# Three float32r passes for a float32 product in the first phase of a two-layer attention kernel

The kernel runs on one core of one Trainium2 chip. The metric is the device time of one execution in microseconds (us); medians are over several executions, and a span is the time between the first and the last instruction of the one execution that was profiled.

## The reference

Two attention layers over an image batch, 8 images of 512 channels and 1024 positions, all float32. The change touches only the q, k, v product of layer 0.

```python
# layer 0
h = group_norm(x)                                    # 32 groups
qkv = einsum('oc,bct->bot', qkv_w, h) + qkv_b        # 1536 x 512 weights
q, k, v = split(qkv.reshape(b * 8, -1, T), 3)        # 8 heads of 64
q, k, v = fake_quant(q), fake_quant(k), fake_quant(v) # 8 bits; the scale comes from
                                                      # min and max of the WHOLE tensor
w = softmax(q^T k / sqrt(64)); a = v w^T
x = x + proj_w a + proj_b
# layer 1: group norm, q/k/v, one head of 512, projection, residual (cut)
```

The quantisation needs the minimum and maximum over the whole batch before any value can be rounded. So the kernel has two phases: phase 1 computes q, k and v of all images, stores them in DRAM and keeps their extremes; phase 2 reads them back, quantises, and does the attention of layer 0 and all of layer 1, image by image. Between them stands a chain: reduce the extremes, compute the scales, load and quantise the first head, find its row maxima (from score matmuls called `sm`), and only then the first score matmul whose result is used (`st`). I call the stretch from the end of the last v matmul to the first `st` the boundary.

## The kernel before

Phase 1 takes one image at a time: statistics and normalisation (`group_norm`, with two tiny averaging matmuls), 64 products of q and k, 32 of v. Weights of layer 1 are merged (`wq` with `wk`, `wv` with `wp`, matmuls `mg`, and small ones for the biases, `mgb`) on TensorE right after phase 1.

```python
for b in range(B):
    if b + 1 < B:
        load_x(b + 1)
    ...                                              # cut: loads of layer 1 weights
    group_norm(xs.pop(b), hn, V_GN0W, V_GN0B, f"a{b}")
    for h in range(HEADS):
        ps = big_ps(f"qkps_{b}_{h}")                 # PSUM, 1024 columns
        for hf in range(NH):
            for cc in range(CC):                     # 4 blocks of 128 channels
                nc.tensor.matmul(ps[:, bass.ts(hf, 512)],
                    lhsT=wqkv[:, cc, h*3*CH : h*3*CH + 2*CH],
                    rhs=hn[:, cc, bass.ts(hf, 512)], start=(cc == 0), stop=(cc == CC - 1))
        nc.vector.tensor_scalar(qk, ps, vec[...], None, ALU.add, ALU.max, accum_out=qkmax[...])
        nc.vector.tensor_reduce(qkmin[...], qk, AX.X, ALU.min)
        nc.sync.dma_start(qk_d[b][h], qk)
    for t in range(NT):
        ...                                          # cut: v, the same with operands swapped
        nc.vector.tensor_add(vt, ps, vb)
        ...                                          # cut: max, min, store
merge_weights()
```

## Time and profile before

4405.49 us in the median of three runs (4390.6 to 4419.51). The stages, from the table of stages that the prediction shows:

| stage | us | length | what sets its end |
|---|---|---|---|
| start, to the first q/k product | 0 to 31.4 | 31 | loads, statistics of image 0 |
| phase 1 | 31.4 to 761.1 | 730 | TensorE, 94% busy |
| boundary | 761.1 to 810.0 | 49 | the merge to 797, beside which the chain of scales is done by 781; then the first maxima |
| phase 2 | 810.0 to 4403.8 | 3594 | TensorE, 92% busy |

One thing about the reading of TensorE rows: records overlap with their neighbours (616 ns in the mean where they start every 429), so a stream is timed from start to start.

### The profile page before, as it was taken

How to read it: one execution, taken by the hardware profiler on the slowest of the kernel's cores; microseconds unless marked ns; L12 is line 12 of the kernel's file. 1: busy time of each engine (PE TensorE's matmuls, PEld its weight loads, DVE VectorE, ACT ScalarE, POOL GpSimd, SP SyncE). 2: the span in 40 equal slices, each digit the busy share in tenths (PEclk: the TensorE clock that was granted, in tenths of full speed). 3: DMA queues.
4: the chain of work that ended last, by engine and by line, in shares of the span. 5: the costliest groups of instructions: out<-in, count | busy, mean ns of one | idle time of the engine just before them, and what ended most of it. 6: DMA issues, size and time to landing. Idle time of an engine off the chain costs nothing.

```text
span 4403.8 us, 26651 instructions
## 1 busy us (share of the span) xinstructions
PE 4049.7 (92%) x10432; PEld 1529.5 (35%) x10432; DVE 1782.4 (40%) x2621; ACT 1051.7 (24%) x1129; POOL 109.0 (2%) x102
## 2 busy tenths in 40 slices
PE   7899999889998899989988998999989989998999
PEld 3344444323432343234322432243224422442244
DVE  4544444554234523452355224522452244324422
ACT  0000000342133312431243123312331243113411
POOL 0000000000000000000000000000000000000000
PEclk9999999899998999899989998999889988999899
DMA  4222212100010101010101010101010100000000
GB/s 186 93 95 91 86 73 85 53 20 29 0 48 15 34 0 48 15 34 0 43 20 34 0 43 20 34 0 43 15 35 4 38 20 15 24 28 26 1 0 19
DMA packets 69678, 161.92 MB, mean 37 GB/s; under 512 B 23216, under 2 KB 23216, under 8 KB 68912
## 3 DMA queue, kind: packets, MB, share of 16 engines
q1 hardware_dynamic: 64032, 135.05, 8.5%
q10 hardware_dynamic: 5520, 25.17, 1.5%
q8 instruction: 82, 1.34, 0.1%
q14 instruction: 44, 0.36, 0.0%
HBM read 92.56 MB, written 67.11 MB: 36 GB/s over the span
## 4 chain that ended last, share of the span: by engine, by line
PE 83%; DVE 7%; ACT 4%; issue 3%; DMA 2%; POOL 0%; SPq 0%; POOLq 0%; ACTq 0%; DVEq 0%
PE av L384 20%; PE o L511 10%; PE s L477 10%; PE qkps L208 9%; PE sm L323 7%; PE qk L452 5%; PE st L395 5%; PE v2ps L464 5%; PE pj L432 4%; PE vps L226 4%; DVE negm L330 3%; PE tp L503 1%; DMA sums<-un 1%; ACT pt L403 1%; DVE q_aug L350 1%
## 5 line engine op out<-in xcount | busy, mean ns | idle before, releaser
L384 PE MATMUL av<-pt,vq 128*65 128x512 f32 x2048 | 1102.9, 666 | 70.6 <-ACT pt L403 70.6
L330 DVE TENSOR_REDUCE negm<-sm 128x1 f32<-128x1024 f32 x512 | 626.3, 1224 | 892.4 <-PE sm L323 891.6
L403 ACT ACTIVATE pt<-st,esc 128x1024 f32<-128x1024 f32 x512 | 569.6, 1114 | 931.7 <-PE st L395 930.4
L384 PEld LDWEIGHTS av<-pt,vq 128*65 128x65 f32 x2048 | 294.5, 151 | 602.1 <-issue 425.5
L208 PE MATMUL qkps<-h,wqkv 128*128 128x512 f32 x1024 | 462.9, 616 | 30.4 <-ACT h L158 30.3
L477 PE MATMUL s<-h,q 128*128 128x512 f32 x1024 | 443.4, 592 | 0.0
L511 PE MATMUL o<-pT,v 128*128 128x512 f32 x1024 | 442.9, 593 | 0.3 <-DVE pT L505 0.3
L323 PE MATMUL sm<-k_aug,q_aug 64*128 64x512 bf16 x1024 | 341.3, 417 | 69.3 <-DVE negm L330 36.7
L395 PE MATMUL st<-q_aug,k_aug 67*128 67x512 bf16 x1024 | 347.7, 415 | 54.0 <-DVE q_aug L350 44.0
L208 PEld LDWEIGHTS qkps<-h,wqkv 128*128 128x128 f32 x1024 | 201.9, 198 | 285.4 <-issue 253.0
L511 PEld LDWEIGHTS o<-pT,v 128*128 128x128 f32 x1024 | 193.9, 190 | 244.5 <-issue 241.1
L477 PEld LDWEIGHTS s<-h,q 128*128 128x128 f32 x1024 | 193.3, 190 | 237.2 <-issue 237.2
L452 PE MATMUL qk<-h,wqk 128*128 128x512 f32 x512 | 240.7, 634 | 29.6 <-ACT h L158 29.6
L158 ACT ACTIVATE h<-h,vec 128x1024 f32<-128x1024 f32 x64 | 68.3, 1137 | 748.4 <-DVE h L154 748.4
L323 PEld LDWEIGHTS <-q_aug 64*128 64x128 bf16 x1024 | 65.1, 96 | 502.4 <-issue 427.4
L432 PE MATMUL pj<-ao,wp 128*128 128x512 f32 x512 | 221.8, 593 | 0.0
L464 PE MATMUL v2ps<-wvp,h 128*128 128x512 f32 x512 | 221.0, 592 | 0.0
L226 PE MATMUL vps<-wqkv,h 128*128 128x512 f32 x512 | 221.0, 592 | 0.0
L471 DVE COPY v<-v2ps 128x512 f32<-128x512 f32 x64 | 44.3, 692 | 415.0 <-PE v2ps L464 415.0
L489 ACT ACTIVATE p<-s,nm 128x1024 f32<-128x1024 f32 x64 | 71.4, 1115 | 546.2 <-DVE nm L486 546.2
L519 DVE SCALAR_TENSOR_TENSOR x<-o,ub,x 128x512 f32<-128x512 f32 x64 | 48.1, 751 | 376.7 <-PE o L511 376.7
L216 DVE TENSOR_SCALAR_CACHE_REDUCE qk<-qkps,vec 128x1024 f32<-128x1024 f32 x64 | 82.1, 1283 | 252.3 <-PE qkps L208 252.3
(113 smaller groups left out, 2207.3 us busy)
## 6 DMA issues: line engine op xcount, KB each, us to landing
qk_d<-qk SPq DMA_DIRECT2D x64, 512.0 KB, 2.6
rqk<-qk_d SPq DMA_DIRECT2D x64, 512.0 KB, 3.5
x<-in_x_dram SPq DMA_DIRECT2D x32, 512.0 KB, 6.1
v_d<-v SPq DMA_DIRECT2D x64, 256.0 KB, 2.0
x<-in_x_dram ACTq DMA_DIRECT2D x8, 2048.0 KB, 7.8
rv<-v_d SPq DMA_DIRECT2D x32, 512.0 KB, 4.2
out_dram<-x SPq DMA_DIRECT2D x16, 1024.0 KB, 4.2
wraw<-in_w_res_dram ACTq DMA_DIRECT2D x4, 1024.0 KB, 8.9
```

The source lines that it names most:

```text
L208: nc.tensor.matmul(ps[:, bass.ts(hf, 512)], lhsT=wqkv[:, cc, h * 3 * CH : h * 3 * CH + 2 * CH], rhs=hn[:, cc, bass.ts(hf, 512)], start=(cc ...
L226: nc.tensor.matmul(ps, lhsT=hn[:, cc, bass.ts(t, P)], rhs=wv_cols[:, cc, :, 2, :], start=(cc == 0), stop=(cc == CC - 1),)
L323: nc.tensor.matmul(ps[:, bass.ts(hf, 512)], lhsT=q_aug[a][0:CH, bass.ts(t, P)], rhs=k_aug[a][0:CH, bass.ts(hf, 512)], start=True, stop=True,)
L330: nc.vector.tensor_reduce(negm[g][:, t : t + 1], ps, AX.X, ALU.max, negate=True)
L384: nc.tensor.matmul(av[hf][0 : CH + 1, :], lhsT=vq[b][:, s, h, :], rhs=pt[:, bass.ts(hf, 512)], start=(s == 0), stop=(s == NT - 1),)
L395: nc.tensor.matmul(ps[:, bass.ts(hf, 512)], lhsT=k_aug[a][:, bass.ts(s, P)], rhs=q_aug[a][:, bass.ts(hf, 512)], start=True, stop=True,)
L403: nc.scalar.activation(pts[s], ps, AF.Exp, scale=esc)
L432: nc.tensor.matmul(ps, lhsT=wp0[:, cc, bass.ts(oc, P)], rhs=src[:, cc, :], start=(cc == 0), stop=(cc == CC - 1),)
L452: nc.tensor.matmul(ps[:, bass.ts(hf, 512)], lhsT=wqk[:, cc, bass.ts(oc, P)], rhs=hn[:, cc, bass.ts(hf, 512)], start=(cc == 0), stop=(cc == ...
L464: nc.tensor.matmul(ps, lhsT=hn[:, cc, bass.ts(t, P)], rhs=wvp[:, cc, :], start=(cc == 0), stop=(cc == CC - 1),)
L477: nc.tensor.matmul(ps[:, bass.ts(hf, 512)], lhsT=qt[:, cc, bass.ts(n, P)], rhs=hn[:, cc, bass.ts(hf, 512)], start=(cc == 0), stop=(cc == C ...
L511: nc.tensor.matmul(ps, lhsT=vt[:, m, bass.ts(dc, P)], rhs=pT[:, m, :], start=(m == 0), stop=(m == NT - 1),)
```

## The change

Intent: a float32 matmul makes four passes through the array (the prediction says from where; in the trace it is two records). Split each operand into a high part that float32r is meant to take exactly, and a rest; three such passes, added up suitably, are meant to give a product of the same accuracy. With x = hi + lo, w = wh + wl and E12 = 2^-12, the sum is (1 + E12) (hi wh + lo wl/E12) + (hi - lo/E12) (wl - E12 wh), which multiplies out to x w; the code calls the last two factors `su` and `ws`, and wl/E12 `wd`. Three passes in place of four is 25% off. To hide the splitting and the group norm behind matmuls, phase 1 now goes by halves of an image, with the next half split and the next image normalised while the present one is multiplied. PSUM, where matmuls leave their results, is given to it in another way (3 x 2 banks), and so is SBUF, the memory for operands; the loads and the merge of the layer 1 weights stand in the program after the first row maxima of phase 2.

```diff
+        def split(i, cc):                      # one half image, one channel block
+            nc.scalar.activation(hi, h, AF.Copy, scale=SHRINK)
+            nc.vector.tensor_sub(lo, h, hi.bitcast(F32))
+            nc.vector.scalar_tensor_tensor(
+                su, lo.bitcast(F32), -1.0 / E12, hi.bitcast(F32), ALU.mult, ALU.add)
+        def product(nm, w, x, swap=False):
+            for part in (0, 1, 2):             # hi*wh, lo*wd -> p1_;  su*ws -> p2_
+                for cc in range(CC):
+                    nc.tensor.matmul(p2_ if part == 2 else p1_, lhsT=a_, rhs=b_, ...)
 # q and k: bias on ScalarE out of PSUM, then one fused add and max
+            nc.scalar.activation(t_, p1_, AF.Identity, bias=..., scale=1.0 + E12)
+            nc.vector.tensor_tensor_reduce(out=qk, in0=t_, in1=p2_, op0=ALU.add,
+                                           op1=ALU.max, accum_out=qkmax[...])
 # v: the bias is a row, added on GpSimd
+            nc.scalar.activation(t_, p1_, AF.Copy, scale=1.0 + E12)
+            nc.gpsimd.tensor_tensor(t_, t_, vb, ALU.add)
+            nc.vector.tensor_tensor_reduce(out=vt, in0=t_, in1=p2_, ...)
 # start: the weights are split too, four quarters of 1536 columns
+            nc.scalar.activation(wh[:, cc, :], raw, AF.Copy, scale=SHRINK)
+            nc.vector.tensor_sub(lo, raw, ...); tensor_scalar(wd, ...); scalar_tensor_tensor(ws, ...)
 # loop
-        for b in range(B):  group_norm(...); 8 heads; 8 tiles of v
+        for i in range(B * NH):                # halves
+            for h in range(HEADS):
+                qk_of(i, h)
+                if nxt and h % 2 == 1:
+                    split(i + 1, h // 2)
+                if hf == 0 and h == 1 and b + 1 < B:
+                    norm(b + 1)
+            for j in range(NT // NH):
+                v_of(i, j)
-    merge_weights()
 ...                                            # cut: phase 2 up to its first row maxima
     put_max(0)
+    merge_weights()                            # with its loads, 5 MB
```

## The prediction

> **What bounds the kernel now.** I read the page first, then the same trace cut into stages, then the timeline at the places where two stages meet. The page gives the frame:
>
> ```profile
> span 4403.8 us, 26651 instructions
> PE 4049.7 (92%) x10432; PEld 1529.5 (35%) x10432; DVE 1782.4 (40%) x2621; ACT 1051.7 (24%) x1129; POOL 109.0 (2%) x102
> L208 PE MATMUL qkps<-h,wqkv 128*128 128x512 f32 x1024 | 462.9, 616 | 30.4 <-ACT h L158 30.3
> L226 PE MATMUL vps<-wqkv,h 128*128 128x512 f32 x512 | 221.0, 592 | 0.0
> ```
>
> TensorE is busy for 92% of the span. The change touches only the two matmul lines of phase 1 (L208 for q and k, L226 for v), 462.9 + 221.0 = 683.9 us, so what it can win is a part of that. The program holds 768 such products and the profile counts 1536: one float32 matmul is two records. The table of stages (columns: window, its length, busy time of PE, PEld, DVE, ACT, POOL, granted clock, DMA share, GB/s) says what limits phase 1, and what is beyond it:
>
> ```profile
> 31.40:761.10 729.70, 686.68 (x1565) 304.82 (x1566) 346.82 (x535) 32.96 (x31) 7.06 (x7) 0.96 0.23 89
> 761.10:797.10 36.00, 36.00 (x129) 20.69 (x127) 13.43 (x34) 13.64 (x20) 0.62 (x2) 0.96 0.58 198
> 797.10:810.00 12.90, 8.99 (x26) 2.74 (x26) 11.28 (x17) 0.00 (x0) 0.00 (x0) 0.50 0.00 0
> 810.00:4403.00 3593.00, 3316.87 (x8712) 1200.22 (x8711) 1398.36 (x2006) 1002.64 (x1076) 96.80 (x79) 0.93 0.07 22
> ```
>
> Phase 1 is the first row: TensorE 94% busy, VectorE under half, DMA under a quarter. It is bound by TensorE. The second row is the weight merge, the third the first row maxima, and the fourth (3593 us) is the attention of both layers. The timeline of the last two images shows the seams:
>
> ```profile
> 675.83 57.88 PE L208 MATMUL qkps<-h,wqkv 128*128 128x512 f32 x128 [3.70 <-ACT h L158]
> ...
> 733.54 27.63 PE L226 MATMUL vps<-wqkv,h 128*128 128x512 f32 x64
> ...
> 761.01 27.63 PE L108 MATMUL mg<-wraw 128*128 128x512 f32 x64
> ...
> 788.48 8.71 PE L120 MATMUL mgb<-vec,wraw 128*128 128x1 f32 x64
> ...
> 797.13 1.89 PE L323 MATMUL sm<-k_aug,q_aug 64*128 64x512 bf16 x4
> ```
>
> The v records start at 733.54 and the merge at 761.01, so 64 records take 27.47 us, 429.2 ns from start to start. (The means of 592 and 616 ns overlap, because matmuls are pipelined; the spacing is what counts.) One image is 192 x 0.4292 = 82.4 us, plus 2.8 us because the first records after the pause run at half clock, plus a pause of some 6.9 us for the group norm: 8 x 85.2 + 7 x 6.9 = 730 us, the row above. The merge (36 us) covers the wait for the quantisation scales: TensorE never stops between 733 and 797.
>
> **What the Trainium skill says.** "FP8 and Floating Point Precision", section TensorE Precision Notes: float32 goes through the array in four passes (high and low parts), and one pass works at about 22 bits. "TensorE: Matmul & The Clock Gate", section Back-to-back issue gap: a warm matmul of N columns takes N/2.4 + 2.5 ns. The trace agrees: two passes of 512 in one record are 1024/2.4 + 2.5 = 429.2 ns, exactly what was measured; so one pass should be 512/2.4 + 2.5 = 215.8 ns. The trace supports single passes at that rate, though only for bfloat16: two st matmuls, each with its own weight load, take 0.44 us (855.28 - 854.84). The same page, section LDWEIGHTS, has about P/1.2 ns for P columns, 107 ns for 128. The float32 transposes agree: 24 of them, each with its own 128-column load, start between 1161.08 and 1163.72, every 110 ns. A load for every pass thus fits behind 215.8 ns. "GPSIMD Engine Reference", section 3.1, puts a two-input tensor_tensor at about 2.6 cycles per element, so 512 x 2.6 / 1.2 = 1.1 us for the new bias add; no trace here shows one of that size.
>
> **The change part by part.** *Matmuls.* Each of the 768 products becomes three single passes, 3 x 215.8 = 647 ns instead of 858 ns. An image has 96 products: 62.2 us instead of 82.4 us; eight images 497 us instead of 659 us, a gain of 162 us. This rests on a float32r pass running at one column per cycle, which no record of this trace shows; that is my choice.
>
> *The group-norm pause.* The order of instructions of the changed program puts the statistics of image b+1 into image b's stream, and its two small averaging matmuls a product apart. The seven pauses of 6.9 us and the half-clock starts (2.8 us each) go: 7 x 9.7 = 68 us. In their place VectorE is fuller. Per image, by durations of the present rows: 24 results with a reduction, some 0.76 us each (the 1024-wide L216 takes 1.33 us to the next operation, less 512 elements at 0.96 GHz, 0.53), and 24 minima of 0.60, together 33; 8 splits of two operations (0.61 and 0.69), 10; the norm, 9 to 10. Sum 52 to 56 us against 62.2 of TensorE: 85 to 90%. In the first half of an image, where the norm falls, it is 31 against 31, and three PSUM buffers bridge two products. I charge 1.5 us a time, 12 us in all, for the lag. ScalarE has 24 x 0.59 + 8 x 0.71 + 4 x 1.14 = 24 us per image, GpSimd 8 x 1.1 = 9: neither binds.
>
> *The start.* The weights are split before the first product: per quarter ScalarE 1.5 us, VectorE two 1536-wide operations of (1536 + 151)/0.96 = 1.76 us and one of about 0.95, so 4 x 4.5 = 18 us on VectorE, in line with 11 us of statistics for two images, 3 of normalisation and the first splits; the averaging matmuls of image 1 also precede the first product. VectorE gets its first data at 11 us and is then nearly full for 35 to 40 us: the stream starts at about 50 us instead of 31.4. Cost 19 us.
>
> *The end of phase 1.* From the end of the last v matmul (761.1) to the first st (810.0) it was 49 us, with the merge hidden in the scale chain (761 to 781) and then TensorE still merging until 797. Now the merge stands after the first maxima on TensorE's queue, and the st matmuls stand after the merge. So: scale chain about 23 us (before 20; the last v now passes through GpSimd and a longer VectorE tail), maxima and their transposes 12, merge 36, of which its first 5 us at half clock add 2.5: 73 us. The five 1 MB weight loads are issued as phase 1 ends; at the 198 to 276 GB/s that the trace reaches they take 20 to 27 us, done before the merge wants them at about 35. Cost 73 - 49 = 24 us. After the first st the order on TensorE is the same in both programs, so 3593 us stay.
>
> *Sum.* 50 + 2.7 (cold start) + 497 + 12 = 562 us to the end of phase 1, + 73 = 635 at the first st, + 3594 = 4229 us of span, + 1.7 us by which the median time exceeds the span = 4231. I add 7 us for what a new stage usually leaves unfilled: **4238 us**, 3.8% less.
>
> **The rivals.** (1) *VectorE becomes the bound of phase 1.* For it: 85 to 90% load in an in-order queue; the fused add-and-max may be slower than I took it (if 0.4 us more each, 62 to 66 us per image, or more); GpSimd shares SBUF access with it. Against it: three PSUM buffers and its 48% now. At 68 us per image phase 1 ends near 600: 4275 us. (2) *Weight loads set the pace.* Each pass brings its own load, and the records show 190 ns for a float32 load of 128 columns, near the 216 of a pass. Against it: these 190 ns lie under other matmuls, and the transposes turn one round in 110 ns. At 260 ns a pass an image is 75 us: about 4335 us, within 2%. (3) *A float32r matmul needs two passes.* Then it is 3 x 429 ns a product, 8 x 124 us, and the kernel is slower: about 4720 us. Against it: then there would be nothing to split for. (4) *The gain is as large as it can be:* a start at 46 us, no lag, a boundary of 65 us: 4208 us.
>
> **Range and chances.** Between (4) and a VectorE bound of moderate size the range is 4205 to 4290 us. The 2% mark is 0.98 x 4405.5 = 4317. Rival 1 does not reach it; rival 2 and a combination of a late start with a bad boundary do. Faster by over 2%: 0.86; within 2%: 0.10; slower: 0.04, almost all of it rival 3.
>
> **What would show it.** In the changed profile: one record per product and pass, 2304 in all, at a spacing of 216 ns in the middle of an image (260 or more: rival 2; 429: rival 3); the busy time of phase 1's matmuls about 500 us; no pause above 2 us between images; VectorE at 85 to 90% in phase 1, with no matmul waiting long for its results (at 97% and over, with long waits for it: rival 1); the first product stream at about 50 us, the end of v near 562, the merge after the first sm, the first st near 635, and then 3593 us. A wait of the merge for its weights, or of the first sm for a slow load of q and k behind them, would make the boundary longer than the 73 us and the prediction too low.

## The result, and the profile after

The changed kernel takes 4245.28 us in the median of four runs (4236.1 to 4256.63), the kernel before 4411.98 on the same chip (four runs, 4390.6 to 4419.51). The ratio is 0.9631, 95% interval 0.9587 to 0.9675: faster by 3.7%. Ratios here are the mean time of one kernel's fast runs over that of the other's of the same rounds, so not quite the ratio of the medians quoted. The result passed as correct; how accurate it is was not measured, and the check is not sharp enough to tell (it also passed a kernel with one of the three passes left out, below). The page of the changed kernel:

```profile
span 4239.2 us, 29270 instructions
PE 3875.0 (91%) x11200; PEld 1660.8 (39%) x11200; DVE 1852.0 (44%) x2953; ACT 1216.4 (29%) x1389; POOL 196.5 (5%) x166
```

768 more records on TensorE, yet 175 us less busy time. The table of stages, cut at the first product, the end of v, the start of the merge and the first `st` (columns as in the prediction: window, length, busy time of PE, PEld, DVE, ACT, POOL, granted clock, DMA share, GB/s):

```profile
43.80:580.60 536.80, 529.54 (x2329) 436.38 (x2329) 397.99 (x845) 186.88 (x282) 93.58 (x71) 1.00 0.31 117
580.60:620.00 39.40, 8.99 (x25) 2.70 (x24) 23.07 (x47) 4.58 (x4) 3.44 (x4) 0.55 0.81 319
620.00:658.30 38.30, 38.30 (x130) 22.32 (x130) 1.15 (x3) 4.69 (x8) 0.00 (x0) 0.90 0.00 0
658.30:4239.20 3580.90, 3296.03 (x8713) 1197.50 (x8713) 1398.11 (x2007) 1007.41 (x1084) 96.85 (x80) 0.94 0.07 22
```

Phase 1 fell from 730 to 537 us and is still TensorE's: 99% busy. The boundary grew from 49 to 78 us: 39 us in which TensorE has nearly nothing to do, then 38 us of merge that nothing hides. Phase 2 has the same instructions; its 13 us less are looked at below. In the middle of an image, four passes of one operand a line, the timeline shows:

```profile
149.02 1.07 PE L184 MATMUL qk<-h,wh 128*128 128x512 f32 x4
149.93 1.07 PE L184 MATMUL qk<-h,wd 128*128 128x512 f32 x4
```

From start to start 0.91 us for four passes; from this row to the one at 183.47 us there are 38 such steps, 34.45/38 = 0.9066 us each: 226.6 ns a pass. And the boundary, lines of TensorE, GpSimd and VectorE (the brackets tell the idle time before and who ended it):

```profile
579.68 1.07 PE L184 MATMUL v<-ws,h 128*128 128x512 f32 x4
...
592.91 0.40 POOL L294 PARTITION_ALL_REDUCE exa<-ext  x1 [9.20 <-issue]
...
600.50 1.86 PE L406 MATMUL sm<-k_aug,q_aug 64*128 64x512 bf16 x4 [19.75 <-ACT k_aug L399]
...
607.13 0.75 DVE L386 TENSOR_SCALAR qi<-rqk,qk_rcp 128x1024 f32<-128x1024 f32 x1 [1.19 <-DMA rqk<-qk_d]
609.92 2.14 PE L406 MATMUL sm<-k_aug,q_aug 64*128 64x512 bf16 x4 [7.56 <-DVE negm L413]
...
620.01 28.90 PE L353 MATMUL mg<-wraw 128*128 128x512 f32 x64
648.75 9.66 PE L365 MATMUL mgb<-vec,wraw 128*128 128x1 f32 x64
658.28 1.01 PE L478 MATMUL st<-q_aug,k_aug 67*128 67x512 bf16 x2
```

So: 19.9 us from the last v to the first `sm`, 19.5 us for the first maxima, 38.3 us of merge. In the scale chain, GpSimd's reduction over partitions starts 9.2 us after VectorE has made its input (583.7); no run asks why. In the maxima VectorE's queue has quantising of v and of the next q and k ahead of the maxima, and the second `sm` group waits 7.56 us for it. VectorE stands idle in this for 1.97, 0.70 and 1.19 us, 3.9 in all, until loads of v, q and k have landed, which run beside the weight loads (DMA share 0.81 over the 39 us); the rest is the quantising itself.

Three questions were left for experiments: why a pass takes 226.6 ns where bfloat16 takes 215.8; what each part of the change is worth; and what still stands in phase 1's way. In the table, the times of each trace that are used below (us; "v end" is the end of the last v record, the last two columns are TensorE's busy time in phase 2 and the median time, or the only one of a single run):

| kernel | first product | v end | first st | phase 2 | PE busy in it | median |
|---|---|---|---|---|---|---|
| before | 31.4 | 761.1 | 810.0 | 3593.8 | 3316.9 | 4411.98 |
| after | 43.8 | 580.7 | 658.3 | 3580.9 | 3296.0 | 4245.28 |
| four passes by halves | 26.6 | 693.7 | 762.5 | 3618.3 | 3341.1 | 4387.14 |
| early merge | 45.7 | 587.8 | 631.2 | 3567.7 | 3287.5 | 4240.24 |
| two passes (not exact) | 43.6 | 450.5 | 532.5 | 3611.2 | 3334.5 | 4145.87 |
| after, again | 43.8 | 579.6 | 658.0 | 3600.3 | 3321.7 | 4260.33 |
| both ends | 36.6 | 581.1 | 624.5 | 3591.6 | 3314.7 | 4216.13 |
| no bias add (wrong) | 43.7 | 571.3 | 649.4 | 3626.2 | 3350.8 | 4277.32 |
| add on VectorE | 43.8 | 571.9 | 650.2 | 3633.5 | 3360.3 | 4279.28 |
| add aside (wrong) | 43.8 | 573.6 | 651.1 | 3601.2 | 3321.5 | 4253.89 |
| both ends, add on VectorE | 36.4 | 564.4 | 614.4 | 3592.2 | 3312.8 | 4211.79 |

### The profile page after: what moved, and what is told of

Read it like the earlier page. It is cut to its first block, busy times and chain, and to the rows that moved or that the text cites. A ratio compares the mean times of both kernels' runs of the same rounds, so it can differ in the third digit from the quotient of the medians.

```text
span 4239.2 us, 29270 instructions
## 1 busy us (share of the span) xinstructions
PE 3875.0 (91%) x11200; PEld 1660.8 (39%) x11200; DVE 1852.0 (44%) x2953; ACT 1216.4 (29%) x1389; POOL 196.5 (5%) x166
## 4 chain that ended last, share of the span: by engine, by line
PE 83%; DVE 8%; ACT 4%; DMA 2%; issue 2%; POOL 1%; POOLq 0%; SPq 0%; ACTq 0%; DVEq 0%
PE av L467 21%; PE o L594 10%; PE s L560 10%; PE qk L184 7%; PE sm L406 7%; PE qk L535 6%; PE st L478 5%; PE v2ps L547 5%; PE pj L515 5%; PE v L184 3%; DVE negm L413 3%; DMA sums<-un 1%; PE tp L586 1%; ACT pt L486 1%; ACT vq L447 1%
## 5 line engine op out<-in xcount | busy, mean ns | idle before, releaser
L467 PE MATMUL av<-pt,vq 128*65 128x512 f32 x2048 | 1089.5, 659 | 70.9 <-ACT pt L486 70.9
L478 PE MATMUL st<-q_aug,k_aug 67*128 67x512 bf16 x1024 | 344.0, 411 | 54.2 <-DVE q_aug L433 43.7
L568 DVE TENSOR_REDUCE nm<-s 128x1 f32<-128x1024 f32 x64 | 78.4, 1224 | 233.1 <-PE s L560 233.1
L478 PEld LDWEIGHTS <-k_aug 67*128 67x128 bf16 x1024 | 69.7, 99 | 276.7 <-issue 270.0
L506 POOL PARTITION_BROADCAST bc<-bc x64 | 86.7, 1354 | 1856.5 <-DMA bc<-rs 1082.2
L535 PEld LDWEIGHTS qk<-h,wqk 128*128 128x128 f32 x512 | 103.8, 205 | 160.3 <-issue 130.0
L203 ACT ACTIVATE t<-qk,vec 128x512 f32<-128x512 f32 x128 | 87.4, 688 | 224.6 <-PE qk L184 196.6
```

Source lines behind the costliest of these rows:

```text
L203: nc.scalar.activation(t_, p1_, AF.Identity, bias=vec[:, V_QKB + h : V_QKB + h + 1], scale=1.0 + E12)
L467: nc.tensor.matmul(av[hf][0 : CH + 1, :], lhsT=vq[b][:, s, h, :], rhs=pt[:, bass.ts(hf, 512)], start=(s == 0), stop=(s == NT - 1),)
L478: nc.tensor.matmul(ps[:, bass.ts(hf, 512)], lhsT=k_aug[a][:, bass.ts(s, P)], rhs=q_aug[a][:, bass.ts(hf, 512)], start=True, stop=True,)
L535: nc.tensor.matmul(ps[:, bass.ts(hf, 512)], lhsT=wqk[:, cc, bass.ts(oc, P)], rhs=hn[:, cc, bass.ts(hf, 512)], start=(cc == 0), stop=(cc == ...
```

## The experiments

### e1_probe: streams of matmuls alone

The kernel does nothing but streams of 96 matmul records, each with its own weight load, and copies x to the output.

```diff
+    probe("ra", wr, mr, 96)              # float32r, 512 columns
+    probe("bf", wb, mb, 96)              # bfloat16
+    probe("fp", w, m, 48)                # float32, two records each
+    probe("rhalf", wr, mr, 96, N=256)
+    probe("bhalf", wb, mb, 96, N=256)
+    probe("rnarrow", wr, mr, 96, M=64)   # 64 weight columns
+    probe("rsame", ...); probe("ralone", ...); probe("rb", wr, mr, 96)
```

> The cost of one float32r pass by itself (the kernel computes nothing useful, its output is a copy of x, wrong on purpose). Streams of 96 matmuls back to back, nothing else on the chip: float32r 128x128 by 512 (ra, rb), the same in bfloat16 (bf), float32 (fp, 48), float32r and bfloat16 with 256 columns (rhalf, bhalf), float32r with a 64-column weight (rnarrow), with the same weight every time (rsame), without accumulation (ralone). The changed kernel showed 226.6 ns from start to start where the prediction had 215.8. Theory 1, the weight load of four-byte data sets the pace: rhalf stays above 190 ns, rnarrow falls to 216, bf is 216 to 220. Theory 2, a fixed extra of some 11 ns in each float32r record: rhalf about 120, rnarrow and rsame 226. Theory 3, the stream of four-byte columns is 5% slower: rhalf about 113, fp above 429. Theory 4, the neighbours in the real kernel slow it: ra is 216.

The timeline, one line a stream; a spacing is the difference of two starts over 96:

```profile
24.58 22.12 PE L83 MATMUL ra<-mr,wr 128*128 128x512 f32 x96
46.54 20.89 PE L83 MATMUL bf<-mb,wb 128*128 128x512 bf16 x96
67.27 41.36 PE L83 MATMUL fp<-m,w 128*128 128x512 f32 x96
108.07 12.06 PE L83 MATMUL rhalf<-mr,wr 128*128 128x256 f32 x96
119.98 10.65 PE L83 MATMUL bhalf<-mb,wb 128*128 128x256 bf16 x96
130.39 22.32 PE L83 MATMUL rnarrow<-mr,wr 128*64 128x512 f32 x96
```

bfloat16 takes 215.9 ns and float32r 228.7 in the first stream, 226.9, 226.7 with the same weights every time and with no accumulation. With 256 columns it is 108.4 and 124.1 ns; 64 weight columns take 230.8. So the extra of some 11 to 16 ns does not scale with the columns, and comes neither from the neighbours in phase 1 nor from the accumulation. The kernel's 226.6 ns is what a float32r stream takes by itself.

### e2_four_pass: the structure by halves without float32r

The changed kernel with plain float32 products, no splits, results taken as before (and a third buffer for x).

```diff
-        wh = p1w.tile([P, CC, 3 * C], F32R, name="wh")           # and wd, ws
+        wh = p1w.tile([P, CC, 3 * C], F32, name="wh")
-            for part in (0, 1, 2):
-                for cc in range(CC):
+            for cc in range(CC):
+                nc.tensor.matmul(p1_, lhsT=a_, rhs=b_, ...)       # a_, b_: wh and x
-                    split(i + 1, h // 2)                          # and the weights' split
-            nc.gpsimd.tensor_tensor(t_, t_, vb, ALU.add)
+            nc.vector.tensor_add(vt, p1_, vb)
```

> The new structure of phase 1 (halves of an image, norm of the next image inside the stream, merge in phase 2) with the old float32 matmuls of four passes; no split. If hiding the norm is worth what I predicted (seven pauses of 6.9 us and the half-clock starts of 2.8 us go, 68 us, less about 9 us of waits for the averaging matmuls), phase 1 ends at 33 + 659 + 9 = about 702 us (before: 761), the boundary still costs 77 us, and the time is about 4368 us, 1% under before. Rival: the norm still stops TensorE as long as before because the averaging matmuls stand in its in-order queue; then the time is before plus the 28 us of the longer boundary, about 4440 us.

4387.14 us, ratio 0.9929 (0.9914 to 0.9944), right result.

```profile
26.55 8.97 PE L163 MATMUL qk<-x,wh 128*128 128x512 f32 x16 [4.15 <-ACT x L118]
...
689.66 4.03 PE L163 MATMUL v<-wh,x 128*128 128x512 f32 x9
```

The last v ends at 693.7 where before it was 761.1, 67 us sooner: 63 of them from a shorter stream (729.7 to 667.1 from first product to end of v), which is what hiding the norm is worth, and 5 from an earlier first product. The boundary is 68.8 us, 20 more than before with the merge behind the maxima, and 9 less than in the changed kernel, where I had expected 77. The 9 us lie in one place: GpSimd's reduction over partitions starts 0.1 us after its input here, and 6.3 us after it in the kernel before, 9.2 in the changed one. In those two a memset stands right before it in GpSimd's queue, after the end of v; here GpSimd had been idle for 157 us. Whether that is the reason is not tested. The rest of the distance to the changed kernel, 693.7 - 580.7 = 113 us, is the three passes with all that they need: the stream from first product to v end is 130 us shorter (667.1 to 536.8) and starts 17 us later. The total came out above the 4368 us that I had expected, though v ended sooner than its 702, because phase 2 took 3618 us in this profile.

### e3_early_merge: the merge back into the scale chain

The layer 1 weights are loaded in the last two images into the tiles of x that come free, and merged inside phase 1's block, behind the last v.

```diff
+            if hf == 0 and b + 2 >= B:
+                load_raws(b + 2 - B, p1)
+        merge_weights(ps_p, ps_g)        # after the last v, PSUM of phase 1
 ...
     put_max(0)
-    merge_weights()
```

> The changed kernel with the merge put back to the end of phase 1: the four weights are loaded during the last image into the x buffers that are free by then, and the merge runs while the scales are worked out. If the boundary is long because the merge stands after the maxima, the first st comes 49 to 52 us after the last v matmul instead of 77.7 us, and the time falls by 26 to 28 us to about 4217 us. Also the wait of the first maxima for the v loads (7 us) should go, as no weight load is beside them. Rival: the scale chain and the loads set the boundary, and only those 7 us go: about 4238 us.

```profile
587.68 27.63 PE L156 MATMUL mg<-wraw 128*128 128x512 f32 x64
...
618.70 1.03 PE L411 MATMUL sm<-k_aug,q_aug 64*128 64x512 bf16 x4
...
631.20 0.58 PE L483 MATMUL st<-q_aug,k_aug 67*128 67x512 bf16 x1 [0.35 <-DVE q_aug L438]
```

The boundary is 43.5 us in place of 77.7: the merge covers the scale chain again, and the maxima take 12 us. Their loads now have the DMA to themselves, and also the time of the merge to land; the run does not tell the two apart. Phase 1 ends 7 us later: its first product comes 1.9 us later, and half of the small `mgb` matmuls slipped into it (3.6 us). The first `st` comes at 631.2, 27 us sooner. The time is 4240.24 us, ratio 0.9618 (0.9601 to 0.9636), which does not stand out from the changed kernel's 0.9631 (0.9587 to 0.9675): I had expected 26 to 28 us less, but 27 us are 0.6%, and phase 2 differs by as much from execution to execution (the five times go from 4200.77 to 4255.94, and the profile is of the fastest).

### e4_two_pass: is VectorE near?

The second of the three passes is dropped (not an exact product).

```diff
-            for part in (0, 1, 2):
+            for part in (0, 2):
```

> The changed kernel without the second of the three passes (wrong result on purpose). Where is VectorE's own limit? If TensorE still bounds phase 1: 768 passes of 226.6 ns less, 174 us, phase 1 ends near 407 us and the time is about 4071 us. If VectorE takes over, as its 398 us of busy time from 44 us on say: phase 1 ends at 445 to 465 us, long waits of matmuls for VectorE's results appear, time about 4120 us.

256 x 3 records of 226.6 ns are 174 us of TensorE; the last v came 130 us sooner. Then TensorE waits, as the view of waits shows (waited for: us in total, times, longest):

```profile
PE v L184 <- DVE qkmax L207: 20.3, 6, 3.4
```

VectorE is 94% busy from 43.6 to 450.5 us (382.9 of 406.9), as the second branch of the expectation had it. So VectorE could carry phase 1 in 407 us, 130 us below the 537 of the changed kernel. VectorE as the bound was not near.

### e5_after_again: the changed kernel unedited, on the chip of the runs below

```diff
 (no edit)
```

> The changed kernel once more, unedited, so that it and the kernel with both ends mended share a chip, and to see whether the length of phase 2 belongs to the kernel or to the execution. By the traces so far phase 1 and the boundary repeat to a microsecond while phase 2, with the same instructions, took from 3568 to 3618 us, and its TensorE busy time from 3288 to 3341 us with the granted clock, while VectorE busy stayed at 1398 to 1399. If it belongs to the execution: first product at 43.8 us, last v matmul ends at 580 to 582, first st at 657 to 660 as in the first trace, and phase 2 anywhere from 3565 to 3620 us; median time 4230 to 4275 us. If it belonged to the program: 3581 us again to within 3 us.

4260.33 us (five runs, 4250.29 to 4268.11), ratio 0.9641 (0.9625 to 0.9657). First product, v end and first `st` repeat to 1.1 us; phase 2 took 3600.3 us where it took 3580.9. So within a kernel its length belongs to the execution. Over all profiles of the table it goes from 3568 to 3634 us, with TensorE's busy time from 3288 to 3360, while VectorE's in the same stretch was always 1398 to 1399: of these two only TensorE differs, with its clock. The mean granted clock of these spans was 0.92 to 0.94.

### e6_both_ends: the start shortened as well

The early merge, and the weights loaded and split by halves of their columns: heads 0 to 3 before the first product, the rest while those are computed. The norm of image 1 also moves in the program, from behind head 1 to behind head 5; its statistics still ran before the first product.

```diff
-        for cc in range(CC):
-            ...                          # cut: split of all 1536 columns
+        load_w(0, nc.scalar)
+        split_w(0)                       # columns of heads 0 to 3
         norm(0)
         load_x(1)
+        load_w(1, nc.sync)
 ...
+                if i == 0 and h == 0:
+                    split_w(1)
```

> The early merge (as in the run of that name) and in addition the weights split by halves of their columns: before the first product only the columns of heads 0 to 3, the others while those heads are computed; the work of norm 1 then fills the waits of norm 0 on VectorE. Theory: the start of the changed kernel is set by VectorE, which was busy from 10 to 44 us without a gap of 1 us. Half of the weight splitting is 4 x 2.2 = 8.8 us less before the first product, so it should start at 34 us (31 to 38) instead of 43.8. Rival: the start is set by the loads of x and of the weights, which are still the same number of bytes for x: then it starts at 40 to 43. With 34: last v matmul at 578 (early merge: 587.7), first st at 621 (early merge 631, changed kernel 658), total 37 us under the changed kernel of the same rounds where phase 2 is equal: ratio to the kernel before 0.953 to 0.96. If the split of the second half of the columns now delays the results of heads 0 to 3, TensorE shows waits of 3 to 6 us near 50 us and the gain at the start is halved.

```profile
36.57 3.27 PE L224 MATMUL qk<-h,wh 128*128 128x512 f32 x7 [0.51 <-ACT h L208]
...
624.45 0.58 PE L505 MATMUL st<-q_aug,k_aug 67*128 67x512 bf16 x1 [0.35 <-DVE q_aug L460]
```

The first product comes 7.2 us sooner than in the changed kernel and 9.1 sooner than with the early merge alone, for 8.8 expected. Fewer bytes of weights come first, too, but in the changed kernel VectorE had no gap of 1 us between 10 and 44 us, so its work on the weights did set the start. The first `st` is at 624.5, 33.6 us ahead of the changed kernel on the same chip. 4216.13 us (six runs, 4187.1 to 4224.4), ratio 0.9536 (0.9514 to 0.9559): its interval lies clear of the 0.9641 (0.9625 to 0.9657) of the changed kernel in the same rounds. This one beats both kernels.

### e7_no_pool_add: without the bias add of v (wrong)

```diff
-            nc.gpsimd.tensor_tensor(t_, t_, vb, ALU.add)
```

> Wrong on purpose: the bias add of v on GpSimd is left out. In the changed kernel the VectorE subtraction of the split (two SBUF inputs, 128x512) took 681 ns in the median but up to 1793 ns, mean 922, and the slow ones lay beside a GpSimd add. Theory: GpSimd's two-input add holds up VectorE instructions with two SBUF inputs. Then no subtraction is over 750 ns here, the mean falls to about 680 and VectorE's busy time in phase 1 by some 64 x 0.24 = 15 us (529.5 to 514). Rival: the slow ones come of something else (ScalarE's writes, the stores of q and k): the mean stays near 920. In both cases phase 1 keeps its length (last v matmul at 579 to 581), since TensorE bounds it; the first sm comes 1 to 2 us sooner after it because the last v passes no GpSimd.

(The check does not see the missing bias.) The first half was met: no subtraction is slow. VectorE's busy time in phase 1 fell by 13 us, from 398.0 to 384.9 (the 529.5 in the expectation is TensorE's, misread). One line's summary (duration min/median/max in ns) in the changed kernel:

```profile
L169 DVE TENSOR_TENSOR h<-x,h x64: 676/681/1793, 44.1 to 522.3; 128x512 fp32r<-128x512 f32 x64
```

and without the add:

```profile
L169 DVE TENSOR_TENSOR h<-x,h x64: 677/685/693, 44.0 to 511.3; 128x512 fp32r<-128x512 f32 x64
```

The other half was a miss, and the useful one: I had expected phase 1 to keep its length, and the last v ended at 571.3, 8 to 9 us sooner. In the changed kernel TensorE waited in phase 1 only for the second averaging matmul of the norms, and VectorE idled before its v results for GpSimd:

```profile
PE gps_a L108 <- DVE gd_a L106: 7.3, 6, 1.2
```

```profile
DVE v L230 <- POOL tv L228: 72.4, 48, 2.4
```

Without the add TensorE waits for nothing in phase 1. Two explanations were left: GpSimd's 1.29 us (median) stand in the way of each v result, and the in-order queue of VectorE with the norm's small operations behind it; or GpSimd disturbs VectorE's two-input operations.

### e9_vector_add and e11_add_aside: in the way, or a disturbance?

Two kernels tell it apart. The first makes the add on VectorE, which has 44 us more to do; the result stays right. The second leaves GpSimd its add at the same place, but into a tile that nobody reads (wrong).

```diff
-            nc.gpsimd.tensor_tensor(t_, t_, vb, ALU.add)
+            nc.vector.tensor_add(t_, t_, vb)                  # e9_vector_add
+            nc.gpsimd.tensor_tensor(aside, t_, vb, ALU.add)   # e11_add_aside
```

> The changed kernel with the bias add of v on VectorE in place of GpSimd; the result stays right. The run without the add missed my expectation: phase 1 did not keep its length, it ended at 571.2 instead of 579.4 to 580.6 us and no matmul waited. So the add, or the engine it stands on, costs phase 1 some 9 us. Theory: it is GpSimd (its 1.3 us in the way of each v result, or its disturbance of VectorE), not the work: then with 64 more VectorE operations of 0.69 us (44 us, VectorE 385 + 44 = 429 of 527 us, 81%) the last v matmul still ends at 571 to 573. Rival: any further 0.7 us per v result in VectorE's queue delays the averaging of the norms in the same way: then 578 us or later. Boundary 77 to 79 us as before. Total 4225 to 4265 us by the phase 2 that comes.

> Wrong on purpose: GpSimd makes the same add on the same data at the same time, but into a tile of its own that nobody reads; VectorE takes the sum without bias. It tells two ways apart in which GpSimd can cost phase 1 its 9 us. Theory, in the way: VectorE's in-order queue stood behind each v result that came 1.3 us late through GpSimd (in the changed kernel VectorE idled 72 us for it, 56 us for TensorE in its place without the add), and the norm's small operations behind those. Then here, as without the add, the last v matmul ends at 571 to 573, though the subtraction of the split stays slow (mean about 900 ns, up to 1.8 us). Rival, disturbance: GpSimd's add slows VectorE operations with two SBUF inputs from 0.68 to up to 1.8 us, and that delays the norm: then the last v ends at 578 to 581 as in the changed kernel. In both the slow subtractions should still be there beside GpSimd adds.

With the add on VectorE the last v ended at 571.9 and TensorE waited for nothing between 47 and 568 us, though VectorE is fuller. The total was above the 4225 to 4265 us expected (below). The table of stages, phase 1 of this kernel:

```profile
43.82:571.29 527.47, 527.47 (x2327) 436.62 (x2328) 424.29 (x908) 186.47 (x282) 7.43 (x7) 1.00 0.32 119
```

With the add aside there is no wait of TensorE between 47 and 568 us either, and v ends at 573.6 (a shade over the 571 to 573 expected), though the disturbance is still there. It fell on the next operation of the split, not on the subtraction as I had written:

```profile
L170 DVE SCALAR_TENSOR_TENSOR h<-h,h x64: 672/680/1190, 45.2 to 515.3; 128x512 fp32r<-128x512 f32 x64
```

So the queue standing behind a v result that comes late through GpSimd is enough to explain the waits. Not fully separated: the disturbance added 64 x (922 - 681) ns = 15 us in the changed kernel and about 7 us here (mean 790 ns), so half of it also went. In time nothing of this shows: with the add on VectorE 4279.28 us, ratio 0.9662 (0.9632 to 0.9693); phase 2 took 3633.5 us in its profile, which is of the slowest of the four runs (4245.91 to 4285.43).

### e10_all_three: both ends, and the add on VectorE

```diff
 (e6_both_ends, with nc.vector.tensor_add(t_, t_, vb))
```

> The kernel with both ends mended and in addition the bias add of v on VectorE; right result. If the add on VectorE frees phase 1 of its waits: first product at 36.6 us as before, last v matmul at 580.9 - 7 = 573 to 575, first st at 616 to 619 (624.5 with both ends alone). Ratio to the kernel before 0.951 to 0.953 where it was 0.9536 [0.9514, 0.9559]; so in the totals hardly beyond the interval, in the trace plain. If VectorE now holds up the second half of the weight split at the start, a wait of 3 us or more shows before 70 us and the gain shrinks to 4 us.

Last v at 564.4, 16.7 us ahead of e6_both_ends and sooner than expected: the waits are gone, and so is half of the small `mgb` matmuls (4 us), which had slipped into phase 1. All of them now come behind the merge, where they cost the boundary 7 us more. First `st` at 614.4, 10 us ahead of e6_both_ends, a little sooner than expected. 4211.79 us (4201.52 to 4226.24), ratio 0.9540 (0.9522 to 0.9559): not to be told from 0.9536. The 10 us are plain in the trace and not in the time.

### e8_probe2 and e12_probe3: what the extra of a float32r pass is not

Again streams alone, with other sizes of data (N), weight columns (M) and rows.

```diff
+    probe("r128", wr, mr, 96, N=128); probe("b128", wb, mb, 96, N=128)
+    probe("f128", w, m, 48, N=128); probe("r384", wr, mr, 96, N=384)
+    mixed("mix", 96); rows("r64", wr, mr, 96, 64); rows("b64", wb, mb, 96, 64)
```

> Wrong on purpose: streams of matmuls alone, 96 records each with its own weight load. The first probe gave 226.8 ns for a float32r record of 512 columns (bfloat16 215.9) and 124.1 for 256 columns (bfloat16 108.4). Theory A, a fixed extra of 11 to 16 ns per float32r record: 384 columns 174 to 179 ns, 128 columns 67 to 72 ns, bfloat16 with 128 columns 56 to 58. Theory B, the extra is a sign that loading float32r weights takes longer than a record of few columns: then 128 columns take 100 to 190 ns, near the load, and 64 rows of weights may be quicker than 128. float32r and bfloat16 records in turn, 512 columns: 221 ns a record if the extra belongs to each float32r record, 227 if to a turn between loads, over 230 if changing the type costs in addition. float32r with 64 rows in place of 128: 226 to 227 (A), nearer 216 if what is loaded matters. The plain stream at the end repeats 226.7.

```profile
48.08 10.83 PE L83 MATMUL r<-mr,wr 128*128 128x128 f32 x96
58.76 5.53 PE L83 MATMUL b<-mb,wb 128*128 128x128 bf16 x96
64.13 10.94 PE L83 MATMUL f<-m,w 128*128 128x128 f32 x96
```

384 columns take 174.3 ns (the next stream starts at 74.82, the one after it at 91.55), as A has it, but 128 columns take 111.3 ns, not 67 to 72: there theory B is right, the load sets the pace. bfloat16 does it in 55.9. 64 rows change nothing (228.1 ns), and float32r and bfloat16 in turn take 460 ns a pair, 17 more than the two streams alone would. That is 230 ns a record, between two of the cases named beforehand: taking turns costs something, but whether by the type or by the loads stays open.

The last probe asks whether the extra comes with a weight load that is not fast.

```diff
+    probe("b64", wb, mb, 96, M=64);  probe("b96", wb, mb, 96, M=96)
+    probe("r96", wr, mr, 96, M=96);  probe("r32", wr, mr, 96, M=32)
+    probe("b64s", ..., M=64, N=128); probe("r64s", ...); probe("b96s", ..., M=96, N=128); probe("r96s", ...)
```

> Wrong on purpose: streams alone, 96 records each. The earlier probes left open what the extra of a float32r record is: 226.8 ns against 215.9 for bfloat16 with 512 columns. The second probe showed that 128-column loads of float32r weights bound at 111 ns a record, where bfloat16 turned over in 56; the Trainium skill, TensorE: Matmul & The Clock Gate, section Weight-path perf modes, has a fast weight load for 128 weights of a type other than float32. Theory L: the extra comes with a load that is not fast. Then bfloat16 with 64 or 96 weight columns, which by that page has no fast load, also takes 225 to 231 ns a record of 512 columns, and with 128 columns of data takes 53 to 60 ns (64 weight columns) or 80 to 85 ns (96). Theory A: the extra belongs to the float32r pass itself: then bfloat16 with 64 and 96 weight columns stays at 216 ns, and float32r stays at 226 to 231 with 96 and 32 weight columns too. If the load of float32r weights sets the pace only for short records, float32r with 128 columns of data takes near 58 ns with 64 weight columns and 84 ns with 96.

(The first two lines hold two streams each, 64 and 96, then 96 and 32 weight columns.)

```profile
67.80 41.76 PE L83 MATMUL b<-mb,wb 128*64 128x512 bf16 x192
109.21 44.68 PE L83 MATMUL r<-mr,wr 128*96 128x512 f32 x192
153.82 5.55 PE L83 MATMUL b64s<-mb,wb 128*64 128x128 bf16 x96
159.30 5.98 PE L83 MATMUL r64s<-mr,wr 128*64 128x128 f32 x96
165.12 5.52 PE L83 MATMUL b96s<-mb,wb 128*96 128x128 bf16 x96
170.45 8.36 PE L83 MATMUL r96s<-mr,wr 128*96 128x128 f32 x96
178.64 22.00 PE L83 MATMUL rb<-mr,wr 128*128 128x512 f32 x96
```

bfloat16 with 64 and 96 weight columns stays at 215.7 ns (41.41/192); float32r with 96 and 32 takes 232.3. Theory A stands: the extra belongs to the float32r record, not to a slow load. For short records the load of float32r weights sets the pace: 60.6, 85.3 and 111.3 ns for 64, 96 and 128 weight columns. Why a float32r record has its extra stays open.

## Why the prediction was right

The total was right (4238 us predicted, 4245 measured, range 4205 to 4290), and so was the mechanism: phase 1 stayed TensorE's, with fewer passes and no pauses. That it came within 7 us is partly luck, for errors cancelled. Step by step:

- *A pass takes 215.8 ns.* This was the step that the prediction marked as its choice, and the term that was mis-sized: 226.6 ns. 2304 records make 522 us in place of 497, 25 us too little. The formula was sound for bfloat16 (215.9 measured); a float32r record has an extra of 11 ns that no record of the kernel before could show. That each pass's load is hidden held.
- *The pauses and cold starts of the norm, 68 us.* Shown: 63 us in the stream by the structure alone (e2_four_pass).
- *12 us of lag and 2.7 us of cold start in the stream.* Their sum, 14.7 us, is what phase 1 had beyond its passes (536.8 - 522.1). That match is luck. The seen waits were 7.3 us, six waits of 1.2 us for an averaging matmul, and without any wait 5.5 us were left (e7: 527.6 - 522.1). I had charged the lag to a full VectorE; VectorE was 74% busy, not 85 to 90 (49.7 us of work an image, not 52 to 56, in an image of 67.1), and the cause was the hop of v through GpSimd (shown by e7, e9 and e11, with the reserve given there). A slip in the working did no harm: 1.33 less 0.53 is 0.80 and not 0.76, but a result with a reduction did take 0.76 us (681 + 81 ns).
- *The start at 50 us.* It was 43.8, so the prediction was 6 us too late. The splitting was sized well: the 1536-wide operations took 1.72 to 1.76 us, where the prediction's 0.96 elements per ns gives 1.76. But VectorE was nearly full for 34 us, not 35 to 40, and the first product started before the rests of its operand were made. That VectorE's weight splitting sets the start is shown by e6_both_ends.
- *The end of v at 562.* 580.7: 25 us of pass spacing, less the 6 of the start.
- *The boundary, 73 us.* 77.7. The scale chain was 19.9 instead of 23 (9.2 of it before GpSimd's reduction starts), the merge 38.3 instead of 38.5, but the first maxima 19.5 instead of 12. Of these 7.5 us, 3.9 are VectorE's waits for v, q and k, loaded beside 5 MB of weights, a danger that the sentence at the end of the prediction came near to (it named a slow load before the first `sm`); the rest is the quantising between the first two `sm` groups, which the merge covered before. With the merge and its loads back in front, the maxima took 12 (e3_early_merge).
- *Phase 2 keeps its length.* Its instructions do. In the profiles it was 13 us shorter than before, which is luck of the execution (3600.3 us in e5_after_again). Together with the 7 us of allowance, this hides most of the 19 us by which v ended late and the 5 us of the boundary.

The rivals: VectorE as the bound was 130 us away (e4_two_pass). Loads as the pace-setter: not at 512 columns, but at 128 they are (111 ns). A float32r matmul of two passes: one pass, as taken. The largest gain (4208 us) is about where the kernel with both ends mended stands, by other means.

What stays open: where the extra of a float32r record comes from, and what makes phase 2's clock differ between executions. Whether kernels differ in it too is not settled: the kernels without any wait of TensorE in phase 1 had phases 2 of 3626 and 3634 us in their profiles, but also of 3592 and 3601. That is no more than a suspicion. Open is also what GpSimd's reduction waits for in the boundary.

## What to carry to other kernels

Measure the pace of a matmul type by itself, with its own weight load, before multiplying it by thousands of records; a formula that fits one type to 0.1 ns missed another by 11. When a stage is moved behind another, look at what used to lie beside it: here 20 of the merge's 36 us lay beside the scale chain, and behind the maxima all 38 count, together with its loads, which run beside those of the next step. And an engine that helps out with a small operation stands in the way of the in-order queue that consumes its result; the same add on the fuller engine let phase 1 end 9 us sooner (571.9 for 580.7). Read gains of a part from the traces of its stage when the rest of the kernel varies by more.

## What the Trainium skill lacked or had wrong

- "TensorE: Matmul & The Clock Gate", section Back-to-back issue gap: N/2.4 + 2.5 ns fits bfloat16 (215.9 ns at 512 columns), but no page has the float32r record, 226.6 to 229.2 ns at 512 columns with 128 weight columns, 174.3 at 384, 124.1 at 256. The section calls the formula that of an isolated matmul and gives 131 ns as sustained for 512 columns; here it is the formula that fits a stream, and 131 ns was not seen for any type.
- The same page, section LDWEIGHTS: P/1.2 ns holds for float32r with 4.6 to 7.3 ns on top (60.6, 85.3, 111.3 ns for 64, 96, 128 columns where loads set the pace). For bfloat16 it does not: 55.5 ns a record with 96 weight columns and 128 columns of data, where it gives 80 and the section Weight-path perf modes has a fast load for 128 weights only.
- "GPSIMD Engine Reference", section 3.1: the estimate of 1.1 us from its 2.6 cycles per element for a two-input add of 512 elements was low; it took 1.29 us in the median. Section 8 names the contention with VectorE instructions with two SBUF inputs, without a size: a 681 ns subtraction took up to 1793 ns beside such an add, and a 680 ns one up to 1190.
